# A mixture-of-experts layer and a state-space layer on one core: the 3x3 convolution on four 64x64 tiles of TensorE, one result row per token, part of softplus on TensorE, a Newton step on VectorE, and new slots for the side work

## The chip, the cores and the metric

The kernel runs on one NeuronCore of a Trainium2 chip. The core has engines that work at the same time, each through its own queue in order: TensorE (PE, matrix products into PSUM), VectorE (DVE), ScalarE (ACT), GpSimdE (POOL) and SyncE (SP, which only issues transfers here). They wait for one another by semaphores. The metric is device time in microseconds (us) of one execution; lower is better.

## The reference

The input is 32 images of 128 channels and 56x56 pixels, all in 32-bit floats. Two layers follow one another.

Layer 0 is a 7x7 depthwise convolution, a normalization over the channels, and a mixture of 8 experts of which each pixel ("token") uses its best two. Each expert is a two-layer network (128 to 512 to 128) with a capacity of 1.25 T/8 tokens. The result is input + normalized convolution + a small factor times the experts' weighted sum.

Layer 1 is what the change is mostly about. Cut to what matters (x is the result of layer 0, per image):

```python
xh = cv1_w @ x + cv1_b                                   # 1x1 convolution
l  = silu(batchnorm(depthwise_3x3(xh)))                  # the branch called lt in the kernel
t  = layernorm(xh over channels)                         # one token per pixel, in row order
xm, z = split(t @ in_proj_w.T)                           # 256 channels each
xm = silu(causal_conv4(xm))
dt, Bm, Cm = split(xm @ x_proj_w.T, [8, 24])             # 8, 16 and 16 columns
dt = softplus(dt @ dt_proj_w.T + dt_proj_b)              # 256 channels
for each token, each of 256 channels, each of 16 states:
    h = exp(dt * A) * h + dt * Bm * xm ;  y += h * Cm
g  = ((y + xm * D) * silu(z)) @ out_proj_w.T
out = x + cv2_w @ concat(l, g) + cv2_b
```

## The kernel before

**Layer 0.** The convolution runs on TensorE with banded weight matrices, and its normalized rows go to a table in memory, `res_d`. A routing stage on VectorE finds each token's two experts and its places. A dispatch stage copies token rows into `buf_d`, sorted by expert, with GpSimdE's indirect transfers (line 415). An expert stage (lines 434 to 496) reads `buf_d` in groups of four blocks of 112 tokens, multiplies, and adds each result row back into `res_d` with an indirect transfer that accumulates (line 464), four a group, 1,120 in all. `res_d` has 2T rows: the first T hold the normalized convolution, to which the result of a token's first choice is added; the other T rows are zeroed by 14 transfers (line 247) and take the second choice. All 1,120 transfers are declared independent of one another, as one group named "back".

**Layer 1** (function `layer1`) is software-pipelined by hand. Its order is kept as written. The work is cut into 224 groups `g` (32 images x 7 strips of 8 rows, 448 tokens) and each group into 16 units, one per state. Unit `u` needs, in this order:

- `db_pool` (line 948, POOL): db = du * Bm for both halves of the channels, 128x896;
- `exp_act` (line 954, ACT): da = exp(dt * A) in two instructions, into one of two PSUM buffers `da`;
- `scan_dve` (line 963, DVE): the recurrence over the 448 tokens of both halves, in place in `da`, or into an SBUF tile `hs` if the unit's number is in `POOL_C`;
- `cmul` (line 969): the product with Cm, on DVE, or for the five units of `POOL_C` on POOL;
- `carry_act` (line 975, ACT): the state at the strip's end is copied into db of the next strip (zeros at an image's last strip);
- `sum_pe` (line 911, PE): the product is added up over the 16 states, on four 64x64 tiles of TensorE at once.

The loop runs over `t`, one unit a step, and each step writes into the queues: POOL `cmul(t-1)` if it is POOL's; ACT `carry(t-1)`; POOL `db(t+4)`; ACT `exp(t+1)`; DVE `scan(t)` and its `cmul(t)`; PE, in odd steps, the sums of units t-3 and t-2; then the step's side work. So ACT is one unit ahead of DVE: `exp(t+1)` has to be done while DVE works on unit t. The number of a step within its group is i = t mod 16.

Side work is everything else of a group. Each piece is put at a fixed offset by `at(offset, function)`: with offset -15, `silus` of group g+1 stands in step i = 1 of group g, and so on. The pieces in their order: `moe_pe` (x + res_d, turned by a permutation), `cv1_pe`/`cv1_act` (the 1x1 convolution into `xh`, and squares for the variance), `var_pe`, `rstd_act` and `rstd_pool` (the inverse deviation, with a Newton step on POOL, lines 752 to 755), `bc_pe`, `te_dve` (normalized tokens, with the last three of the strip before copied on POOL, line 777), `xm_pe` (four products for each half, line 785), `silus` (lines 801 to 818: switch ACT's table, silu of xm, silu of the lt branch, silu of z, switch back), `px_pe`, `dt_pe`, the steps of softplus (`sp_abs`, `sp_exp`, `sp_r` on DVE, `sp_ln`, `sp_sub` on POOL at line 873, `sp_add` on DVE at line 877), `du_pool`, `lt_pe` (the 3x3 convolution as nine products with diagonal 128x128 matrices, line 890) and `lt_act` (line 898). When the 16 sums are done, `yz_dve` (line 903, i = 2, ahead of the step's scan) and `out_pe`, `out_act` finish the group.

PSUM is fully used: two `da` buffers of two banks, one accumulator `py` of two banks, and two banks that all other products take in turn (`mm_tile`); a product waits until the reader of the product two before it is done.

## Time and profile before

| what | value |
|---|---|
| time, median of 3 runs | 17951.65 us (17951.25 to 17956.85) |
| profiled execution | 17990.1 us, its span 17988.1 us, mean granted TensorE clock 0.872 |
| convolution, routing, dispatch (to the first expert group at 4552 us) | about 4550 us |
| experts (first to last line-464 transfer, 4572 to 6570 us) | about 2000 us |
| layer 1, first scan (6643 us) to the end | 11345 us, 50.6 us for each of 224 groups |
| DVE, ACT, POOL, PE busy between 12000 and 15000 us | 2774, 2159, 2883, 2679 of 3000 us |

A profile line of a group of instructions names line, engine, operation, output and inputs, number, busy time, mean duration in ns, and the idle time ahead of it with what ended that. A line of the timeline has start, duration, engine, line, operation, and in brackets the idle time before it and what ended it. Durations of one engine overlap a little, so the pace of an engine is read from start to start.

### The profile page before, as it was taken

How to read it: one execution, taken by the hardware profiler on the slowest of the kernel's cores; microseconds unless marked ns; L12 is line 12 of the kernel's file. 1: busy time of each engine (PE TensorE's matmuls, PEld its weight loads, DVE VectorE, ACT ScalarE, POOL GpSimd, SP SyncE). 2: the span in 40 equal slices, each digit the busy share in tenths (PEclk: the TensorE clock that was granted, in tenths of full speed). 3: DMA queues.
4: the chain of work that ended last, by engine and by line, in shares of the span. 5: the costliest groups of instructions: out<-in, count | busy, mean ns of one | idle time of the engine just before them, and what ended most of it. 6: DMA issues, size and time to landing. Idle time of an engine off the chain costs nothing. (4 is left out here: it accounts for less than half of the span.)

```text
span 17988.1 us, 212727 instructions
## 1 busy us (share of the span) xinstructions
PE 13659.5 (76%) x75556; PEld 7243.9 (40%) x75556; DVE 12454.2 (69%) x9483; ACT 9672.7 (54%) x18570; POOL 14710.8 (82%) x9375
## 2 busy tenths in 40 slices
PE   4887120000899988888888888888888888888888
PEld 3887100000677753333333333333333333333333
DVE  1766750000111139999999999999999999999999
ACT  2333000000344447777777777777777777777776
POOL 1333127777788879999999999999999999999999
PEclk8898555555999999999999999999999999999999
DMA  9778712222455545555555555555555555555554
GB/s 224 206 206 207 170 53 82 86 82 69 68 68 68 67 85 165 166 166 164 165 165 165 165 166 165 166 166 164 164 165 165 165 165 165 166 164 164 165 165 155
DMA packets 1567881, 2633.82 MB, mean 146 GB/s; under 512 B 145935, under 2 KB 1012603, under 8 KB 1562720
## 3 DMA queue, kind: packets, MB, share of 16 engines
q1 hardware_dynamic: 1368160, 2464.60, 46.8%
q0 software_dynamic: 198656, 155.62, 5.9%
q8 instruction: 595, 9.75, 0.2%
q14 instruction: 470, 3.85, 0.1%
HBM read 2231.69 MB, written 426.81 MB: 148 GB/s over the span
## 5 line engine op out<-in xcount | busy, mean ns | idle before, releaser
L948 POOL TENSOR_TENSOR db<-du,bb 128x896 f32<-128x896 f32 x3584 | 7416.5, 2092 | 0.1
L963 DVE TENSOR_TENSOR_SCAN da<-da,db 128x898 f32<-128x898 f32 x2464 | 4978.1, 2020 | 86.9 <-ACT da L954 86.8
L954 ACT ACTIVATE da<-dt,aneg 128x449 f32<-128x449 f32 x7168 | 4578.4, 639 | 584.0 <-DVE hs L963 244.6
L911 PE MATMUL py<-prod,ident 64*64 64x448 f32 x28672 | 3472.0, 599 | 116.3 <-POOL prod L969 104.4
L969 DVE TENSOR_TENSOR prod<-da,cb 128x896 f32<-128x896 f32 x2464 | 2689.7, 1092 | 196.7 <-issue 3.6
L969 POOL TENSOR_TENSOR prod<-hs,cb 128x896 f32<-128x896 f32 x1120 | 2321.2, 2073 | 389.2 <-issue 333.2
L963 DVE TENSOR_TENSOR_SCAN hs<-da,db 128x898 f32<-128x898 f32 x1120 | 2262.0, 2020 | 247.9 <-ACT db L975 210.6
L464 POOL DMA_INDIRECT res_d<-ys,xb x1120 | 1650.4, 1474 | 371.8 <-issue 304.6
L415 POOL DMA_INDIRECT buf_d<-xg,slot x1568 | 1535.9, 980 | 486.0 <-issue 476.7
L492 ACT COPY xc<-ept 128x448 f32<-128x448 f32 x280 | 149.0, 532 | 3010.7 <-DMA xb<-buf_d 2033.2
L911 PEld LDWEIGHTS py<-prod,ident 64*64 64x64 f32 x28672 | 981.7, 141 | 1941.7 <-issue 1118.7
L890 PE MATMUL p_l<-xh,dwd 128*128 128x448 f32 x4032 | 1748.1, 580 | 0.0
L490 PE MATMUL ept<-ident,xb 112*128 112x112 f32 x1120 | 200.0, 260 | 2032.7 <-DMA xb<-buf_d 2032.7
L785 PE MATMUL p_xm<-te,wk 128*128 128x448 f32 x3584 | 1415.8, 546 | 0.0
L412 DVE COPY xg<-gate 128x28 f32<-128x28 f32 x56 | 11.5, 232 | 1792.4 <-DMA buf_d<-xg,slot 1792.4
L456 DVE TENSOR_TENSOR ys<-py,b2t 112x512 f32<-112x512 f32 x280 | 193.6, 691 | 1521.6 <-PE py L451 1477.8
L890 PEld LDWEIGHTS p_l<-xh,dwd 128*128 128x128 f32 x4032 | 794.8, 208 | 958.5 <-issue 957.1
L451 PEld LDWEIGHTS py<-w2t,hh 128*112 128x112 f32 x8960 | 1031.1, 177 | 163.2 <-issue 114.8
L451 PE MATMUL py<-w2t,hh 128*112 128x128 f32 x8960 | 1094.9, 275 | 0.0
L175 PE MATMUL pc<-xc,toep 112*112 112x112 f32 (+1 forms) x8192 | 986.6, 280 | 108.0 <-ACT toep L164 66.1
L204 POOL TENSOR_TENSOR xa<-xa,lng 112x896 f32<-112x896 f32 x128 | 278.5, 2175 | 951.0 <-DVE xa L201 584.4
L735 PE MATMUL p_var<-mean_w,sq 128*112 128x1 f32 x1792 | 318.3, 299 | 906.5 <-ACT sq L720 906.5
(227 smaller groups left out, 19612.3 us busy)
## 6 DMA issues: line engine op xcount, KB each, us to landing
bb<-bc_d SPq DMA_DIRECT2D x1792, 448.0 KB
cb<-bc_d SPq DMA_DIRECT2D x1792, 448.0 KB
toep<-toep_d SPq DMA_DIRECT2D x448, 392.0 KB
xg<-res_d SPq DMA_DIRECT2D x56, 1792.0 KB
yg<-res_d SPq DMA_DIRECT2D x448, 224.0 KB
buf_d<-zero SPq DMA_DIRECT2D x14, 4550.0 KB
xb<-buf_d SPq DMA_DIRECT2D x280, 227.5 KB
xt<-in_x SPq DMA_DIRECT2D x32, 1568.0 KB
```

The source lines that it names most:

```text
L175: nc.tensor.matmul(pc[:, c, :, lo:hi], lhsT=tp[c // 2][:, c % 2, 6 - 2 * o : 8 - 2 * o, :], rhs=s4[:, c, :, lo + o - 1 : hi + o - 1], star ...
L415: apart(nc.gpsimd.indirect_dma_start(out=buf_d[:, :], out_offset=bass.IndirectOffsetOnAxis(ap=slots[k][:, q, p0 + j : p0 + j + 1], axis=0) ...
L451: nc.tensor.matmul(py[:, j, :], lhsT=hh[:, k, j * TT : (j + 1) * TT], rhs=w2t[:, k, :], start=k == 0, stop=k == KF - 1,)
L464: apart(nc.gpsimd.indirect_dma_start(out=res_d[:, :], out_offset=bass.IndirectOffsetOnAxis(ap=xb[:, j, C + 1 : C + 2].bitcast(I32), axis=0 ...
L735: nc.tensor.matmul(p[:TT, j : j + 1], lhsT=sq[:, j * TT : (j + 1) * TT], rhs=mean_w[:, 0:1], start=True, stop=True)
L785: nc.tensor.matmul(p[:, :CH1], lhsT=s["wk"][:, k, hs], rhs=d["te"][:, k : k + CH1], start=k == 0, stop=k == DC - 1 and not first,)
L890: nc.tensor.matmul(d["p_l"][:, :CH1], lhsT=s["dwd"][:, t, :], rhs=d["xh"][:, dy : dy + ROWS1, dx : dx + HW], start=t == 0, stop=t == 8,)
L911: nc.tensor.matmul(st[g]["py"][h * HD : (h + 1) * HD, r, :CH1], lhsT=lhsT(rs, h), rhs=rhs[rs, h, :], start=start, stop=stop,)
L948: nc.gpsimd.tensor_tensor(dbv[i][:, :, 1:], st[g]["du"], units[u].pop("bb"), ALU.mult)
L954: nc.scalar.activation(da[:, h * W1 : (h + 1) * W1], st[g]["dt"][:, h, :], AF.Exp, scale=s["aneg"][:, h, i : i + 1])
L963: nc.vector.tensor_tensor_scan(hs, da, dbs[i], 0.0, ALU.mult, ALU.add)
L969: eng.tensor_tensor(w["prod"], w["hs"][:, :, 1:], w.pop("cb"), ALU.mult)
```

## The change

1. `res_d` has T rows. Both choices of a token are added into the same row. The 14 zeroing transfers are gone, and the accumulating transfers are independent only within one expert (`back{e}`): those of expert e follow those of expert e-1. `fetch` reads one row per token, and `moe_pe` has 4 products instead of 8 besides the one for x.
2. `lt_pe` works on four 64x64 tiles: each tap has four products of a 64x64 diagonal block with 4 of the 8 image rows (224 columns), into two PSUM buffers; `lt_act` reads them with four instructions of 64x224, with the scale and bias turned to match (`bnt`).
3. Softplus: relu + ln are added on TensorE (`sp_pe`, two products with the identity for each half, four in all), and DVE subtracts the rounding rest from PSUM, one half at a time (`sp_sub`). POOL's subtraction and DVE's addition are gone.
4. The Newton step and the copy of three columns of `te` go from POOL to DVE.
5. `POOL_C` is now 2, 5, 8, 12, 14, `prod` has six buffers instead of five, and most of the side work has another slot: the silu phase moves from i = 1 to i = 0, `xm_pe` to 14 and 15, `sp_ln` to 7, `lt_pe` to 12 and 13, `lt_act` to 14, ahead of `xm_pe`.

```diff
-POOL_C = (0, 3, 7, 11, 14)
+POOL_C = (2, 5, 8, 12, 14)
...
-        res_d = dram.tile([2 * T, C], F32, name="res_d")
+        res_d = dram.tile([T, C], F32, name="res_d")
...
-        res_t = res_d.rearrange("(k p) c -> p k c", p=TT)
-        for k in range(COLS, 2 * COLS, 64):
-            nc.sync.dma_start(out=res_t[:, k : k + 64, :], in_=zero[:, :, :C].to_broadcast([TT, 64, C]))
...
-                nc.gpsimd.iota(bi, pattern=[[128 * TT, QB], [1, TT]], base=k * T, channel_multiplier=TT)
+                nc.gpsimd.iota(bi, pattern=[[128 * TT, QB], [1, TT]], base=0, channel_multiplier=TT)
...
-                        in_=ys[:, j, :], in_offset=None, bounds_check=2 * T - 1, oob_is_err=False, compute_op=ALU.add,
-                    ), "back")
+                        in_=ys[:, j, :], in_offset=None, bounds_check=T - 1, oob_is_err=False, compute_op=ALU.add,
+                    ), f"back{e}")
...
+            bnt = wp.tile([128, 2, 2], F32, name="bnt")
+            for k in range(2):
+                for r in range(2):
+                    for j, v in enumerate((bbi, bsc)):
+                        nc.scalar.copy(bnt[k * HD : (k + 1) * HD, r, j : j + 1], v[r * HD : (r + 1) * HD, :])
...
-            d["yg"] = two.tile([TT, TPC1, 2, C], F32, name="yg")
-            for k in range(2):
-                r = k * T + t0
-                nc.sync.dma_start(
-                    out=d["yg"][:, :, k, :], in_=res_d[r : r + CH1, :].rearrange("(j p) c -> p j c", p=TT)
-                )
+            d["yg"] = two.tile([TT, TPC1, C], F32, name="yg")
+            nc.sync.dma_start(
+                out=d["yg"], in_=res_d[t0 : t0 + CH1, :].rearrange("(j p) c -> p j c", p=TT)
+            )
...
-                for k in range(2):
-                    nc.tensor.matmul(
-                        p[:, j * TT : (j + 1) * TT], lhsT=yg[:, j, k, :], rhs=perm,
-                        start=False, stop=k == 1 and j == TPC1 - 1,
-                    )
+                nc.tensor.matmul(
+                    p[:, j * TT : (j + 1) * TT], lhsT=yg[:, j, :], rhs=perm, start=False, stop=j == TPC1 - 1
+                )
...
-        def rstd_pool(g):
+        def rstd_dve(g):
...
-            nc.gpsimd.tensor_tensor(w, r, r, ALU.mult)
-            nc.gpsimd.tensor_tensor(w, w, v, ALU.mult)
-            nc.gpsimd.tensor_scalar(w, w, -0.5, 1.5, ALU.mult, ALU.add)
-            nc.gpsimd.tensor_tensor(r, r, w, ALU.mult)
+            nc.vector.tensor_tensor(w, r, r, ALU.mult)
+            nc.vector.tensor_tensor(w, w, v, ALU.mult)
+            nc.vector.tensor_scalar(w, w, -0.5, 1.5, ALU.mult, ALU.add)
+            nc.vector.tensor_tensor(r, r, w, ALU.mult)
...
-                nc.gpsimd.tensor_copy(te[:, : DC - 1], st[g - 1]["te"][:, CH1:])
+                nc.vector.tensor_copy(te[:, : DC - 1], st[g - 1]["te"][:, CH1:])
...
-        def sp_sub(g):
-            d = st[g]
-            nc.gpsimd.tensor_tensor(d["u"], d["u"], d.pop("e"), ALU.subtract)
-
-        def sp_add(g):
-            d = st[g]
-            nc.vector.tensor_tensor(d["dt"][:, :, 1:], d["dt"][:, :, 1:], d.pop("u"), ALU.add)
+        def sp_pe(g, h):
+            d = st[g]
+            d[f"p_sp{h}"] = p = mm_tile("p_sp")
+            for k, v in enumerate((d["dt"][:, :, 1:], d["u"])):
+                nc.tensor.matmul(p[:, :CH1], lhsT=ident, rhs=v[:, h, :], start=k == 0, stop=k == 1)
+
+        def sp_sub(g, h):
+            d = st[g]
+            nc.vector.tensor_tensor(
+                d["dt"][:, h, 1:], d.pop(f"p_sp{h}")[:, :CH1], d["e"][:, h, :], ALU.subtract
+            )
...
-                d["p_l"] = mm_tile("p_l")
+                d["p_l"] = [mm_tile("p_l") for r in range(2)]
+            R = ROWS1 // 2
             for t in ts:
                 dy, dx = divmod(t, 3)
-                nc.tensor.matmul(
-                    d["p_l"][:, :CH1], lhsT=s["dwd"][:, t, :], rhs=d["xh"][:, dy : dy + ROWS1, dx : dx + HW],
-                    start=t == 0, stop=t == 8,
-                )
+                for r in range(2):
+                    rs = slice(r * HD, (r + 1) * HD)
+                    for k in range(2):
+                        nc.tensor.matmul(
+                            d["p_l"][r][k * HD : (k + 1) * HD, : CH1 // 2], lhsT=s["dwd"][rs, t, rs],
+                            rhs=d["xh"][rs, dy + k * R : dy + (k + 1) * R, dx : dx + HW], start=t == 0, stop=t == 8,
+                        )
...
-            d["lt"] = two.tile([C, CH1], F32, name="lt")
-            nc.scalar.activation(d["lt"], d.pop("p_l")[:, :CH1], AF.Identity, bias=s["bbi"], scale=s["bsc"])
+            lt = d["lt"] = two.tile([C, CH1], F32, name="lt")
+            ps = d.pop("p_l")
+            for r in range(2):
+                rs = slice(r * HD, (r + 1) * HD)
+                for k in range(2):
+                    ks = slice(k * HD, (k + 1) * HD)
+                    nc.scalar.activation(
+                        lt[rs, k * CH1 // 2 : (k + 1) * CH1 // 2], ps[r][ks, : CH1 // 2], AF.Identity,
+                        bias=s["bnt"][ks, r, 0:1], scale=s["bnt"][ks, r, 1:2],
+                    )
...
-            w["prod"] = three.tile([128, 2, CH1], F32, name="prod", bufs=5)
+            w["prod"] = three.tile([128, 2, CH1], F32, name="prod", bufs=6)
...
-        at(-35, moe_pe)
-        at(-34, moe_act)
+        at(-30, moe_pe)
+        at(-29, moe_act)
...
-        at(-22, rstd_pool)
-        at(-21, bc_pe)
-        at(-20, te_dve)
-        at(-17, xm_pe, 0)
-        at(-16, xm_pe, 1)
-        at(-15, silus)
-        at(-14, px_pe)
-        at(-13, px_act)
+        at(-23, rstd_dve)
+        at(-22, bc_pe)
+        at(-21, te_dve)
+        at(-2, lt_act)
+        at(-18, xm_pe, 0)
+        at(-17, xm_pe, 1)
+        at(-16, silus)
+        at(-15, px_pe)
+        at(-14, px_act)
         at(-12, dt_pe)
         at(-11, sp_abs)
         at(-10, sp_exp)
         at(-9, sp_r)
-        at(-8, sp_ln)
-        at(-7, sp_sub)
-        at(-6, sp_add)
+        at(-9, sp_ln)
+        at(-7, sp_pe, 0)
+        at(-6, sp_sub, 0)
+        at(-6, sp_pe, 1)
+        at(-5, sp_sub, 1)
         at(-5, du_pool)
-        at(-6, lt_pe, range(0, 5))
-        at(-5, lt_pe, range(5, 9))
-        at(-4, lt_act)
-        work.setdefault(DS * G - 15, []).append((silus, G))
+        at(-4, lt_pe, range(0, 5))
+        at(-3, lt_pe, range(5, 9))
+        work.setdefault(DS * G - 16, []).append((silus, G))
```

More of the change, by code (lines that the diff above doesn't have):

```diff
@@ L62, in tile_kernel @@
         buf_d = dram.tile([E * CAP, RW], F32, name="buf_d")
-        res_d = dram.tile([2 * T, C], F32, name="res_d")
+        res_d = dram.tile([T, C], F32, name="res_d")
         zero = const.tile([TT, 1, RW], F32, name="zero")
         nc.gpsimd.memset(zero, 0.0)
-        nc.gpsimd.memset(zero[:, :, C + 1].bitcast(I32), 2 * T)
+        nc.gpsimd.memset(zero[:, :, C + 1].bitcast(I32), T)
         ident = const.tile([128, 128], F32, name="ident")
@@ L436, in tile_kernel, with products @@
             todo = []
-            def products(g, xb, xc, w1t, w2t, b1t, b2t):
+            def products(e, g, xb, xc, w1t, w2t, b1t, b2t):
                 hh = eb.tile([128, KF, GT * TT], F32, name="hh")
@@ L494, in tile_kernel @@
                         products(*todo.pop())
-                    todo.append((g, xb, xc, w1t, w2t, b1t, b2t))
+                    todo.append((e, g, xb, xc, w1t, w2t, b1t, b2t))
             products(*todo.pop())
@@ L645, in layer1 @@
     mm_tile, res_d, x_d, out_d = s["mm_tile"], s["res_d"], s["x_d"], s["out_d"]
-    perm, T = s["perm"], s["T"]
+    perm = s["perm"]
     G = N * NQ1
```

## The prediction

> **What bounds the kernel now.** I began with the busy time of the engines in a stretch of layer 1 (core total; the columns are stretch, length, then PE, weight loads, DVE, ACT, POOL, TensorE clock, DMA share, GB/s):
>
> ```profile
> 12000.00:15000.00 3000.00, 2679.03 (x13541) 1145.26 (x13542) 2774.47 (x1836) 2158.96 (x4307) 2883.30 (x1676) 0.94 0.54 165
> ```
>
> POOL is busiest (96%), DVE next (92%). Which of them sets the pace is told by the waits between 8000 and 17000 us, some 178 groups (microseconds in total, times, longest):
>
> ```profile
> DVE yz L903 <- PE py L911: 262.1, 178, 2.2
> POOL prod L969 <- issue: 260.5, 319, 1.5
> ...
> ACT da L954 <- DVE hs L963: 193.6, 152, 1.6
> ...
> DVE hs L963 <- ACT db L975: 164.8, 157, 1.4
> ...
> DVE da L963 <- ACT da L954: 68.9, 152, 0.8
> ...
> DVE hs L963 <- POOL te L777: 2.6, 8, 0.3
> ```
>
> DVE waits for PE and ACT, some 2.95 us a group, and for POOL practically never. POOL in turn waits before its products; the timeline of POOL shows them starting just as DVE's scan ends. So the pace is DVE's own work plus its waits for PE and ACT, and POOL, full as it is, follows. The DVE timeline of one group shows the work and the waits:
>
> ```profile
> 12002.23 2.02 DVE L963 TENSOR_TENSOR_SCAN hs<-da,db 128x898 f32<-128x898 f32 x1
> ...
> 12011.31 1.09 DVE L969 TENSOR_TENSOR prod<-da,cb 128x896 f32<-128x896 f32 x1
> 12013.74 1.09 DVE L903 TENSOR_TENSOR yz<-py,zs 128x896 f32<-128x896 f32 x1 [1.34 <-PE py L911]
> ...
> 12018.97 2.03 DVE L963 TENSOR_TENSOR_SCAN hs<-da,db 128x898 f32<-128x898 f32 x1 [1.07 <-ACT db L975]
> ...
> 12030.22 2.02 DVE L963 TENSOR_TENSOR_SCAN hs<-da,db 128x898 f32<-128x898 f32 x1
> 12032.16 1.07 DVE L865 SCALAR_TENSOR_TENSOR sp_e<-sp_u,sp_e 128x896 f32<-128x896 f32 x1
> 12033.67 2.04 DVE L963 TENSOR_TENSOR_SCAN da<-da,db 128x898 f32<-128x898 f32 x1 [0.45 <-ACT da L954]
> ...
> 12052.71 2.02 DVE L963 TENSOR_TENSOR_SCAN hs<-da,db 128x898 f32<-128x898 f32 x1
> ```
>
> First and last row are unit 14 of two groups: 50.48 us. From start to start a unit with its product takes 3.11 us, a unit whose product is POOL's 1.94, sp_r, sp_add and yz 1.0 each, te 0.53. Work: 11 x 3.11 + 5 x 1.94 + 3 x 1.0 + 0.53 = 47.4. The rest, 3.0, is three stalls: 2.4 around ACT's silu phase (1.34 + 1.07), 0.45 before unit 8, and small gaps. The second shows a mechanism that matters below; the ACT timeline:
>
> ```profile
> 12030.86 0.14 ACT L975 COPY db<-da 128x2 f32<-128x2 f32 x1
> 12032.27 1.31 ACT L954 ACTIVATE da<-dt,aneg 128x449 f32<-128x449 f32 x2 [1.27 <-DVE hs L963]
> ```
>
> exp(8) was put into the buffer that scan(7) reads, not the one unit 6 had left, so it starts only as scan(7) ends, and scan(8) starts 3.45 us after scan(7) did (30.22 to 33.67) instead of 1.94. sp_r fills 1.0 of the 1.5.
>
> **The change part by part** (per group; there are 224).
>
> *DVE's work.* sp_add goes (-1.0). Two halves of sp_sub come, each like te (448 columns from PSUM): 2 x 0.55. The four Newton instructions depend on one another; such small ones in the preparation of layer 1 follow at 0.19 if dependent (lines 558 to 560) and at 0.07 if not: 0.75, bounds 0.3 and 1.1. The copy of `te` 0.1. Sum +0.95, bounds +0.5 and +1.4.
>
> *POOL's work.* Gone: 2.04 (line 873), about 1.85 from the first Newton instruction to the next db, 0.15 (line 777). Worth nothing by itself: DVE lost 2.6 us in 9000 to POOL.
>
> *The buffers of exp.* In the built order of the changed program exp(6) waits for scan(5) and exp(9) for scan(8), in 191 of 224 groups (those of an image's last strip, whose carry is zeros, wait for the products of units 4 and 7 instead). No DVE work stands between the scans now, since sp_r follows unit 7. Each place takes 3.45 instead of 1.94: +1.5 twice. ACT then lags: from scan(5) as zero, exp(6) 2.05, sp_abs 3.3 to 5.4 (four at 0.515), exp(7) 5.5, sp_exp and its sum to 8.55; scan(6) 3.45, scan(7) 6.88 (0.3 late), sp_r to 11.0; exp(8) 8.75, cv1_act to 11.3, sp_ln (moved here) 12.1; scan(8) 11.0, exp(9) 13.05, scan(9) 14.45. DVE's work in that is 11.1: stalls 3.3 against 0.45, +2.9. In the 32 last strips only ACT's lateness is left, about 1.25: +0.8. Behind the waiting exps stand sp_abs and carry(7), and cv1_pe and var_pe wait for them; both have over 2 us to spare.
>
> *lt on tiles.* The rows have no tile product of 224 columns. Four of 448 at once (line 911) take 0.83 a set; half the columns take between 0.42 and 0.83. My estimate is 0.46, as stream time halves and 0.08 of overhead stays (the value nearest to the row that is of the same form): nine taps 4.1 instead of 7.1 (12039.49 and 12046.15, 10 and 8 instructions). moe_pe saves 0.9, sp_pe adds four products at 0.78, 3.1. PE's total stays at about 43 of 50 us; it matters only through xm_pe.
>
> *The silu phase.* Now at step 0. lt starts after te and sp_sub's second half on DVE (both PSUM buffers are theirs), at the start of scan(12); with 4.1 for lt and 1.7 for sums it ends 5.8 later, ahead of lt_act, which ACT reaches 6.6 after scan(12). xm_pe now needs the PSUM buffers that lt_act reads: its first half starts 7.3 after scan(12), 3.1; sums 1.7; second half 3.1, ending 15.1 after scan(12), which is 5.0 after unit 15 (1.94 + 3.11 + 1.94 + 3.11 = 10.1). ACT: exp(1) 0.3 after unit 15, table 1.55 to 2.85, silu xm to 3.4, waits for xm's second half to 5.1, silus and z to 7.5, table 8.8, exp(2) 9.0, scan(2) 10.4. DVE's work in between is two units and yz, 7.2: stall 3.1 to 3.2 against 2.4, +0.7. The sums before yz now follow z on PE, but end 8.5 after unit 15, inside this stall. If xm were in time, ACT alone would set 8.7: stall 1.5, -0.9. If lt gains nothing from tiles, all this is 2.5 later.
>
> *lt_act.* Row: one instruction of 448 columns has a pace of 0.62; copies of 56 columns have 0.13 and others of 448 0.515, so by estimate 224 cost 0.295 and four 1.18. It stands after exp(15) and ends before exp(0) is due: hidden by unit 14, and if late it adds to the line above. "TensorEngine Tiling (Array Packing)" of the Trainium skill, PSUM Bottleneck, says that tiling speeds up TensorE but not the emptying of PSUM. By that alone the reading would stay at 0.62 and release xm 0.28 earlier; the rows say that it nearly doubles.
>
> *The other moves.* moe_pe, now 1.8 us, stands at step 2 behind px_pe and ahead of dd and the sums of units 0 and 1; out_pe then ends 5.3 us after scan(3) starts, dt_pe 1.8 later, and sp_abs needs it 2.4 later still, after the late exp(6). bc_pe waits for DVE's Newton step after unit 9, the second sp_pe for the first sp_sub after unit 10; behind them are sums and lt, which start no later than te and the second sp_sub allow. While xm_pe waits for lt_act, sums of units 12 and 13 stand behind it, needed only by yz. SP issues one `yg` transfer less a group; SP held up nothing. A sixth `prod` buffer: DVE waited once, 0.5 us, for one. All nothing; their cover is DVE's own work of 3.1 us a step, and with it gone each would cost what it is late.
>
> *Outside layer 1.* The zeroing ran at 1912 to 2103 us beside the routing on DVE, and SP then waited 404 us for routing: worth 0 to 30 us (DVE waited 30.7 for row stores at the end of the convolution), I take 10. The first add of an expert now waits for the last of the one before: the last of all landed about 1.8 us after POOL had issued it (6570.95 to 6572.75), so about 1.5 seven times, with the expert's other adds behind it on POOL; six `ys` buffers keep DVE and PE going. POOL's adds take 7.03 of each 7.13 us of the PE-bound stage, so little of it is made up: +10. Preparation, first and last group: as before.
>
> Sum: 192 groups x (0.95 + 2.9 + 0.7) + 32 x (0.95 + 0.8 + 0.7) = 874 + 78 = 952 us, less 10, plus 10: 950. The profiled execution (17990, span 17988) would go to 18940; it was 38 above the median of the runs, so the time is 17952 + 950 = 18900.
>
> **Rivals.** *A, PE becomes late* (15%): tile products of 224 columns are bound by weight loads and issue, or run at a lower clock. For it: in the trace, after PE idled 4.27 us, 16 tile products took 3.26 us instead of 1.73, and I expect several gaps of 2 to 3 us in steps 7 to 12. Against: each gap is shorter than that. With +2.5: 18900 + 560 = 19460. *B, the silu stall shrinks* (23%): xm is ready when ACT wants it, as in the profile, where ACT waits 5.2 us for it in 178 groups together. Against: lt_act now stands before xm. -0.9 for +0.7: 18900 - 360 = 18540. *C, faster, by POOL* (4%): if the full POOL queue is the true limit and the DVE waits only mirror it, a group falls to DVE's work of 48.35, -2.1 x 224: 17480. It decides if all stalls left are under 2.1 us a group; the two exp waits alone are 3.0, so the program's waits would have to be met in time, and the same one now is not (152 times 1.27). *D, parts cancel* (2%): 17950.
>
> **How the numbers follow.** The forecast itself has 56%: 18900, its own range 18700 to 19150. The lowest bound of the slower cases is 0.5 + 2.6 - 0.9 = 2.2 in 192 groups, 18360; the highest 1.4 + 3.1 + 0.7 + 2.5 = 7.7, about 19600. I give 18440 to 19460. A measurement tells 0.2% (36 us) from no change: faster 0.045, same 0.015, slower 0.94.
>
> **What would show it.** In the profile after: scan(5) to scan(6) and scan(8) to scan(9) 3.45 apart, with exp waiting for the scan; ACT waiting over 1 us for xm; line-900 products near 4 us a group; POOL with 6 us or more idle in each group; a group of 55 us. I am wrong if DVE's stalls stay near 3 us, or if lt takes 7 us.

## The result, and the profile after

The changed kernel takes 19794.04 us (median of 3 runs, 19790.33 to 19802.44), 1.1026 times the kernel before (95% interval 1.1004 to 1.1047). The forecast was 18900 in a range of 18440 to 19460: slower was right, but the loss is 1842 us and not 950. Its profiled execution has a span of 19800.5 us.

The same stretch of layer 1 as shown of before (length; then PE, weight loads, DVE, ACT, POOL, clock, DMA share, GB/s):

```profile
12000.00:15000.00 3000.00, 2410.88 (x14409) 1044.61 (x14408) 2620.28 (x1880) 1935.40 (x3859) 2256.69 (x1143) 0.87 0.43 138
```

POOL went from 2883 to 2257 us busy, 48.5 to 44.1 us a group (the forecast took 4.0 off), and the kernel gains nothing by it. DVE looks less busy than before (2774), but a part of its 2620 us is no work, as will be seen. TensorE's granted clock is lower, 0.87 against 0.94, and it was busy for 80% of the time instead of 89%. A group took 50.5 us; from unit 8 of one group to unit 8 of the next it is now 58.67.

Where DVE and POOL wait, between 8000 and 17000 us (153 groups; total, times, longest):

```profile
DVE yz L921 <- PE py L929: 430.5, 153, 5.1
DVE da L981 <- ACT da L972: 430.4, 427, 1.8
DVE hs L981 <- ACT db L993: 102.8, 134, 1.1
...
POOL du L887 <- DVE dt L880: 1273.8, 152, 8.8
```

The second line is the stall by exp's buffers (before: 68.9 in 178 groups), the first and third are the silu phase. ACT's timeline has both causes: exp waits for the scan, and in the silu phase ACT waits for the second half of xm, which TensorE starts late because its first half waits for `lt_act` (line 913) to read the buffers (the last fence is TensorE's):

```profile
12054.47 1.31 ACT L972 ACTIVATE da<-dt,aneg 128x449 f32<-128x449 f32 x2 [1.77 <-DVE hs L981]
...
12088.43 2.17 ACT L913 ACTIVATE lt<-p_l,bnt 64x224 f32<-64x224 f32 x4
...
12097.73 0.63 ACT L802 ACTIVATE xm<-p_xm,c1b 128x448 f32<-128x448 f32 x1 [2.22 <-PE p_xm L786]
```

```profile
12089.55 3.27 PE L786 MATMUL p_xm<-te,wk 128*128 128x448 f32 x8 [1.92 <-ACT lt L913]
```

POOL now stands idle 8.4 us a group for DVE. The timeline of DVE shows both stalls as forecast, 3.45 us from the scan of unit 8 to that of unit 9 and 2.68 + 0.77 around yz, and behind the product of unit 9 something that was not:

```profile
12063.52 2.02 DVE L981 TENSOR_TENSOR_SCAN hs<-da,db 128x898 f32<-128x898 f32 x1
12066.97 2.04 DVE L981 TENSOR_TENSOR_SCAN da<-da,db 128x898 f32<-128x898 f32 x1 [1.43 <-ACT da L972]
12069.09 1.09 DVE L987 TENSOR_TENSOR prod<-da,cb 128x896 f32<-128x896 f32 x1
12070.10 1.59 DVE L753 TENSOR_TENSOR rw<-r 112x4 f32<-112x4 f32 x1
12071.72 1.99 DVE L754 TENSOR_TENSOR rw<-rw,v 112x4 f32<-112x4 f32 x1
12073.75 0.17 DVE L755 TENSOR_SCALAR rw<-rw 112x4 f32<-112x4 f32 x1
12073.95 0.16 DVE L756 TENSOR_TENSOR r<-r,rw 112x4 f32<-112x4 f32 x1
...
12101.17 1.09 DVE L921 TENSOR_TENSOR yz<-py,zs 128x896 f32<-128x896 f32 x1 [2.68 <-PE py L929]
12103.03 2.03 DVE L981 TENSOR_TENSOR_SCAN hs<-da,db 128x898 f32<-128x898 f32 x1 [0.77 <-ACT db L993]
```

Lines 753, 754 and 756 are the same operation on 4 columns, yet take 1.59, 1.99 and 0.16 us. No idle time is shown before them: the wait is inside the instruction. POOL's timeline over the same stretch:

```profile
12067.55 6.14 POOL L966 TENSOR_TENSOR db<-du,bb 128x896 f32<-128x896 f32 x3
```

Three products db, 2.05 us each, end at about 12069.6, 12071.7 and 12073.7. Line 753 ends with the second, line 754 with the third, and then POOL has nothing to do and line 756 is quick. The means over all groups say the same, and in some groups line 755 waits too (number, busy time, mean ns):

```profile
L754 DVE TENSOR_TENSOR rw<-rw,v 112x4 f32<-112x4 f32 x153 | 305.0, 1993 | 5.3
L753 DVE TENSOR_TENSOR rw<-r 112x4 f32<-112x4 f32 x153 | 218.3, 1427 | 0.0
L866 DVE SCALAR_TENSOR_TENSOR sp_e<-sp_u,sp_e 128x896 f32<-128x896 f32 x152 | 216.8, 1426 | 0.0
...
L755 DVE TENSOR_SCALAR rw<-rw 112x4 f32<-112x4 f32 x153 | 66.2, 433 | 5.2
L756 DVE TENSOR_TENSOR r<-r,rw 112x4 f32<-112x4 f32 x153 | 24.9, 163 | 5.2
```

DVE's time per group, from the totals of its instructions and waits, divided by 178 groups before and 153 after:

| us a group | before | after | difference | forecast |
|---|---|---|---|---|
| Newton step on DVE | 0 | 4.02 | +4.02 | +0.75 |
| sp_add, or the halves of sp_sub and te's copy | 1.15 | 1.37 | +0.2 | +0.2 |
| sp_r | 1.07 | 1.43 | +0.36 | 0 |
| wait for exp (units 6, 7, 9; before: 8) | 0.39 | 2.81 | +2.4 | +2.6 |
| silu phase: waits before yz and the next scans | 2.53 | 3.57 | +1.0 | +0.7 |
| sum | | | +8.0 | +4.25 |

The measured difference is 1842/224 = 8.2 us a group. (The forecast of 2.6 is 2.9 in 192 groups and 0.8 in 32.)

### The profile page after: what moved, and what is told of

Same layout as the page of the kernel before. It is cut to its first block, busy times and chain, and to the rows that moved or that the text cites. A ratio compares the mean times of both kernels' runs of the same rounds, so it can differ in the third digit from the quotient of the medians.

```text
span 19800.5 us, 237405 instructions
## 1 busy us (share of the span) xinstructions
PE 14124.6 (71%) x87652; PEld 7511.8 (38%) x87652; DVE 13481.3 (68%) x10795; ACT 10009.0 (51%) x19249; POOL 13723.4 (69%) x8063
## 5 line engine op out<-in xcount | busy, mean ns | idle before, releaser
L929 PE MATMUL py<-prod,ident 64*64 64x448 f32 x28672 | 3540.4, 614 | 18.6 <-POOL prod L987 11.5
L987 POOL TENSOR_TENSOR prod<-hs,cb 128x896 f32<-128x896 f32 x1120 | 2163.5, 1932 | 1386.0 <-PE p_moe L698 701.1
L929 PEld LDWEIGHTS py<-prod,ident 64*64 64x64 f32 x28672 | 1051.0, 148 | 2068.9 <-issue 1567.4
L887 POOL TENSOR_TENSOR du<-dt,xm 128x896 f32<-128x896 f32 x224 | 432.2, 1930 | 1908.4 <-DVE dt L880 1882.5
L786 PE MATMUL p_xm<-te,wk 128*128 128x448 f32 x3584 | 1477.0, 555 | 325.4 <-ACT lt L913 323.3
L993 ACT COPY db<-da 128x2 f32<-128x2 f32 x2112 | 335.4, 159 | 2349.7 <-DVE prod L987 2342.8
L763 PE MATMUL p_bc<-ident,r 112*128 112x112 f32 x1792 | 430.5, 418 | 1073.7 <-DVE r L756 1073.7
L786 PEld LDWEIGHTS p_xm<-te,wk 128*128 128x128 f32 x3584 | 645.9, 190 | 1076.6 <-issue 712.9
```

The source lines that it names most:

```text
L763: nc.tensor.matmul(p[:, j * TT : (j + 1) * TT], lhsT=r[:, j : j + 1].to_broadcast([TT, 128]), rhs=ident[:TT, :TT], start=True, stop=True,)
L786: nc.tensor.matmul(p[:, :CH1], lhsT=s["wk"][:, k, hs], rhs=d["te"][:, k : k + CH1], start=k == 0, stop=k == DC - 1 and not first,)
L887: nc.gpsimd.tensor_tensor(d["du"], d["dt"][:, :, 1:], d["xm"], ALU.mult)
L929: nc.tensor.matmul(st[g]["py"][h * HD : (h + 1) * HD, r, :CH1], lhsT=lhsT(rs, h), rhs=rhs[rs, h, :], start=start, stop=stop,)
L987: eng.tensor_tensor(w["prod"], w["hs"][:, :, 1:], w.pop("cb"), ALU.mult)
```

## The experiments

Ratios are to the kernel before, run beside each kernel on the same chip; 0.01 of ratio is 180 us, or 0.80 us for each of the 224 groups. Where a kernel is an edit of the changed one, it is compared with that one's ratio of 1.1026. Two theories stand against each other at first: P, that the Newton step's instructions on DVE wait for POOL's instruction under way, and D, that they cost what was forecast and the loss lies elsewhere.

### The Newton step

**e1: back on POOL**, all four instructions, at the same place of the changed kernel.

```diff
-            nc.vector.tensor_tensor(w, r, r, ALU.mult)
+            nc.gpsimd.tensor_tensor(w, r, r, ALU.mult)
...
```

> The changed kernel, with the four Newton instructions back on POOL, in the same place of the order. Theory P (on VectorE the two tensor_tensor whose inputs all lie in SBUF wait for the POOL instruction that is under way): all of the 3.7 us that VectorE spends on them leaves each group, 224 x 3.7 = 830 us, so 18960 us; and POOL, which now idles 8.4 us a group, has room for its 1.85. Rival D (four small dependent instructions cost 0.75 as forecast, the rest of the loss is TensorE and its lower clock): 19794 - 170 = 19620. Rival S (POOL's Newton step stands behind long products and makes bc and te late): no gain, 19800 or more.

Measured: 18917.08 us, ratio 1.0514 (1.0497 to 1.0532). That is 4.1 us a group less than the changed kernel, all that lines 753 to 756 took. Theories D and S fall. On POOL each of the four took 0.20 us.

**e2: the same step on DVE, one input in PSUM.** This keeps engine, place and count, and changes only where r lies.

```diff
-            nc.scalar.activation(d["r"], d["r"], AF.Exp, scale=-0.5)
+            nc.scalar.activation(p[:TT, 64 : 64 + TPC1], d["r"], AF.Exp, scale=-0.5)
...
-            nc.vector.tensor_tensor(w, r, r, ALU.mult)
-            nc.vector.tensor_tensor(w, w, v, ALU.mult)
+            nc.vector.tensor_tensor(w, rp, v, ALU.mult)
+            nc.vector.tensor_tensor(w, rp, w, ALU.mult)
             nc.vector.tensor_scalar(w, w, -0.5, 1.5, ALU.mult, ALU.add)
-            nc.vector.tensor_tensor(r, r, w, ALU.mult)
+            nc.vector.tensor_tensor(r, rp, w, ALU.mult)
```

> The changed kernel, with the Newton step still on VectorE and in its place, but the first estimate r is written to PSUM, so that each of the three tensor_tensor has one input in PSUM and one in SBUF (w = r*v, w = r*w, r*w; as many instructions as before). Theory P: nothing waits for POOL any more, the step falls from some 3.7 us to 0.75 at most, 224 x 2.9 = 650 us less: 19140 us. Rival D (the time is the instructions' own, or their dependence): unchanged, 19794 within 100. Rival S (the slot of PSUM that r now holds longer makes bc late): slower than 19794.

Measured: 19341.89 us, ratio 1.0750 (1.0732 to 1.0768), 2.2 us a group less, where P had said 2.9. The groups of DVE in this kernel tell why:

```profile
L756 DVE TENSOR_SCALAR rw<-rw 112x4 f32<-112x4 f32 x159 | 169.5, 1066 | 5.5
L757 DVE TENSOR_TENSOR r<-p_var,rw 112x4 f32<-112x4 f32 x159 | 25.7, 162 | 5.5
L755 DVE TENSOR_TENSOR rw<-p_var,rw 112x4 f32<-112x4 f32 x159 | 25.7, 162 | 5.5
L754 DVE TENSOR_TENSOR rw<-p_var,v 112x4 f32<-112x4 f32 x159 | 24.1, 152 | 0.0
```

The three with an input in PSUM never wait: 152 to 162 ns in all 159 groups. The one with a single input, input and output both in SBUF, takes over: 1066 ns in the mean, 174 at the least. So one input and one output in SBUF can be enough to wait; two inputs there are not needed.

**e6: no instruction left that has only SBUF operands.**

```diff
             nc.vector.tensor_tensor(w, rp, v, ALU.mult)
-            nc.vector.tensor_tensor(w, rp, w, ALU.mult)
-            nc.vector.tensor_scalar(w, w, -0.5, 1.5, ALU.mult, ALU.add)
-            nc.vector.tensor_tensor(r, rp, w, ALU.mult)
+            nc.vector.scalar_tensor_tensor(w, w, -0.5, rp, ALU.mult, ALU.mult)
+            nc.vector.scalar_tensor_tensor(r, w, 1.5, rp, ALU.add, ALU.mult)
```

> The changed kernel with the Newton step on VectorE in three instructions, each with one input in PSUM (w = r*v, w = -0.5*w*r, r = (w + 1.5)*r with r in PSUM): the instruction with one input and a constant, which still waited (median 1.2 us) when the other three no longer did, is gone. Theory P: it was waiting for POOL too; three instructions of 0.16 without a wait, 1.2 us a group less than 19342: 19070 us. Rival D (it costs that by itself, or a wait goes to the next one): 19342, or 0.17 a group less, 19300.

Measured: 19244.09 us (19083.76 to 19255.9), ratio 1.0656 (1.0580 to 1.0732). The three took 152, 158 and 157 ns in the mean; none waits, and the whole step takes 0.47 us instead of 4.02. The time is another 0.8 us a group lower than in e2 (the interval is wide); the wait before yz is 0.1 us a group larger.

The page "SBUF — State Buffer" of the Trainium skill, section "Who interferes with whom", says that VectorE and GpSimd share one pair of SBUF ports under an exclusive lock, held for a whole instruction: a VectorE instruction with two SBUF inputs contends with a GpSimd instruction that reads SBUF, and so can `tensor_scalar` and copies, in a mode that uses both ports. These three runs agree with it, in both kinds (1.99 against 0.16 us; 1.07 against 0.17 us).

**e4: the step on DVE alone, in the kernel before** (lines 752 to 755 from `nc.gpsimd` to `nc.vector`, nothing else).

> The kernel before, with nothing changed but the engine of the Newton step: VectorE instead of POOL. Theory P: two of its instructions wait for the POOL instruction under way, 1 to 2 us each, and VectorE sets the pace, so 3 to 3.8 us a group: 17952 + 670 to 850, 18620 to 18800 us. Rival D: 0.75 a group, 18120 us. Rival G (POOL set the pace, and gains 1.85 a group): 17550 to 17950.

Measured: 18323.64 us, ratio 1.0183 (1.0166 to 1.0200): +1.5 us a group, between D and P. The mechanism is P's, the amount is not:

```profile
L753 DVE TENSOR_TENSOR rw<-rw,v 112x4 f32<-112x4 f32 x172 | 323.8, 1882 | 5.9
L752 DVE TENSOR_TENSOR rw<-r 112x4 f32<-112x4 f32 x172 | 55.9, 325 | 0.0
```

With the other two (0.17 and 0.16) this makes 2.5 us a group. The first instruction mostly finds POOL between two products (its median is 152 ns). And 1.4 us come back: the wait before yz, 262.1 us in 178 groups before, is 4.2 here, as DVE reaches yz later, while that before the following scans rises from 1.06 to 1.56 a group. The same step thus costs 1.5 us in the one kernel and 4.1 in the other.

### The two buffers of exp

**e3: POOL's products in the old units.**

```diff
-POOL_C = (2, 5, 8, 12, 14)
+POOL_C = (0, 3, 7, 11, 14)
```

> The changed kernel with the products on POOL in units 0, 3, 7, 11, 14 again instead of 2, 5, 8, 12, 14. In the built order exp(8) then waits for scan(7), and neither exp(6) for scan(5) nor exp(9) for scan(8): one such place instead of two. Theory B (each place costs 1.5 us, and sp_r stands in the one that is left): 1.5 for the place that goes and 1.0 for sp_r in the other, 2.5 us a group, 19794 - 560 = 19230 us. Rival O (ACT's lateness and the silu phase take it back): 19600 to 19800.

Measured: 19636.18 us, ratio 1.0914 (1.0896 to 1.0932), 0.9 us a group less, where B had said 2.5. The wait for exp did go, from 430.4 to 72.4 us. But 2.6 us of waits for TensorE came in its place:

```profile
DVE yz L921 <- PE py L929: 697.5, 155, 6.2
DVE dt L880 <- PE p_sp L876: 142.1, 155, 1.0
```

4.5 us a group before yz against 2.8, and 0.9 before the second half of sp_sub: TensorE isn't early enough for a DVE that comes earlier, as rival O had it. These waits are more than the 2.3 us of stalls that went. What made the kernel faster all the same is that DVE's instructions meet POOL's less: sp_r is back at 1.07 us (from 1.43), and the Newton step takes 3.3 us instead of 4.0.

**e5: the buffers in turn.** Units stay where they are; only the choice of buffer changes.

```diff
-            da = units[u]["da"] = pda.tile([128, 1024], F32, name="da")
+            da = units[u]["da"] = pda.tile([128, 1024], F32, name="da", tag=f"da{u % 2}", bufs=1)
```

> The changed kernel, with one difference: the two PSUM buffers of exp are given to even and odd units in turn, so that in the built order no exp waits for the scan of the unit just before it. Theory B: both stalls of 1.43 us on VectorE go, 2.9 us a group, 19794 - 640 = 19150 us. Rival O (units 6 to 9 come earlier, but the silu phase, which waits for TensorE, does not, and takes it back as it did with the products of POOL moved): 19550 to 19750 us, with VectorE's wait before yz 1.5 us a group or more above the 2.8 of the changed kernel.

Measured: 19970.48 us (19823.97 to 19974.78), ratio 1.1060 (1.0985 to 1.1134): nothing is gained, and neither theory had that. The stall is gone (22.7 us left of 430.4, and 78.3 of other waits in its place), and the silu phase is as it was (2.9 a group before yz). What grew are DVE's instructions in SBUF:

```profile
L866 DVE SCALAR_TENSOR_TENSOR sp_e<-sp_u,sp_e 128x896 f32<-128x896 f32 x153 | 443.5, 2899 | 0.0
L755 DVE TENSOR_SCALAR rw<-rw 112x4 f32<-112x4 f32 x153 | 306.9, 2006 | 5.2
L754 DVE TENSOR_TENSOR rw<-rw,v 112x4 f32<-112x4 f32 x153 | 305.2, 1995 | 5.3
```

sp_r from 1.43 to 2.90, line 755 from 0.43 to 2.01, line 753 down to 0.46: 2.1 us of 2.2 gained are waited again, now behind POOL. Starting earlier, DVE meets more of POOL's products.

**e10: both**, e5's buffers and e6's Newton step.

> The changed kernel with two things: the three-instruction Newton step on VectorE that never waits, and the two buffers of exp in turn. Theory B2 (the buffers' stalls are 2.8 us a group; alone, their end only brought sp_r and the Newton step under POOL's instructions): with the Newton step out of that, 2.8 go and sp_r gives 1.9 back, 0.9 a group, 19240 - 200 = 19040 us, sp_r at a mean of 2.5 to 3 us. Rival O (the silu phase takes what is left too): 19200 to 19300, sp_r at a mean near 1.1.

Measured: 18872.04 us, ratio 1.0489 (1.0471 to 1.0506), 1.3 us a group below e6 (0.7 to 2.0 by e6's interval), a little more than the 0.9 of theory B2. sp_r takes 2.89 us in the mean, as B2 said. So of the 2.8 us a group that the stalls had, a part can be had, once the Newton step is out of POOL's way.

**e11: the same in the kernel before**, where one stall of 0.45 us is left.

> The kernel before with the two buffers of exp in turn, nothing else. Theory B: the stall of 0.45 us before unit 8 goes, 154 + 27 of 224 groups, 17990 - 85 = 17905 us. Rival K (sp_r, which now starts earlier against POOL's long instructions, waits for one of them, 0.5 to 1.9 us, as it did in the changed kernel): 18050 to 18300 us, with sp_r at a mean above 1.5 us.

Measured: 18098.37 us, ratio 1.0059 (1.0042 to 1.0075), slower. K holds, with another instruction than the one it named: sp_r stays at 1067 ns; sp_add, which also has both inputs in SBUF, rises from 1159 to 1603, and the waits around the silu phase by 0.4 us together.

### What the parts on TensorE are worth

**e7: lt not on tiles**, in the changed kernel (functions `lt_pe` and `lt_act` as before, slots as changed).

```diff
-                        nc.tensor.matmul(
-                            d["p_l"][r][k * HD : (k + 1) * HD, : CH1 // 2], lhsT=s["dwd"][rs, t, rs],
-                            rhs=d["xh"][rs, dy + k * R : dy + (k + 1) * R, dx : dx + HW], start=t == 0, stop=t == 8,
-                        )
+                nc.tensor.matmul(
+                    d["p_l"][:, :CH1], lhsT=s["dwd"][:, t, :], rhs=d["xh"][:, dy : dy + ROWS1, dx : dx + HW],
+                    start=t == 0, stop=t == 8,
+                )
```

> The changed kernel with lt not on tiles but as before (nine products of 448 columns into one bank, one instruction for lt_act), in its new place of the order. Theory L (lt on tiles is what keeps the silu phase short): lt takes 7.1 us instead of 3.7 and xm ends 2 to 3 us later, 19794 + 450 to 670 = 20240 to 20460 us. Rival T (the wait is for the buffer that lt_act reads, and one short lt_act gives it back sooner; or lt lies in other stalls): 19600 to 19900 us.

Measured: 20481.21 us, ratio 1.1354 (1.1275 to 1.1434): 2.6 us a group slower, as L said and as the forecast had it for this case (2.5). The timeline of TensorE in this kernel, then in the changed one:

```profile
12030.08 4.03 PE L895 MATMUL p_l<-xh,dwd 128*128 128x448 f32 x10
12035.70 3.27 PE L895 MATMUL p_l<-xh,dwd 128*128 128x448 f32 x8
```

```profile
12082.54 2.07 PE L900 MATMUL p_l<-xh,dwd 64*64 64x224 f32 x40
12085.94 1.69 PE L900 MATMUL p_l<-xh,dwd 64*64 64x224 f32 x32
```

7.3 us against 3.8 for the nine taps. The Newton step and sp_r are as in the changed kernel (4.0 and 1.42 us), so the loss is not theirs. It is in the waits: ACT now waits for lt itself, 4.1 us a group (595.4 us in 146 groups; 0.1 a group in the changed kernel), and DVE for what ACT then does late, 2.4 us a group:

```profile
DVE da L968 <- ACT db L980: 350.5, 131, 3.0
```

**e13: softplus' sum on TensorE alone**, in the kernel before.

```diff
-        at(-7, sp_sub)
-        at(-6, sp_add)
+        at(-8, sp_pe, 0)
+        at(-7, sp_sub, 0)
+        at(-7, sp_pe, 1)
+        at(-6, sp_sub, 1)
```

> The kernel before with one part of the change alone: sp_pe and sp_sub in halves (sp_pe at steps 8 and 9, sp_sub at 9 and 10) in place of sp_sub on POOL and sp_add on VectorE. As forecast (VectorE's work +0.1 us a group, POOL's 2 us worth nothing): 17990 + 0 to 40. Rival C (POOL's load sets the pace): 1 us a group less, 17770. Rival T (3 us more of TensorE at steps 8 and 9 make bc and lt late, as te's wait for bc in the mix showed): 18100 to 18400.

Measured: 18553.82 us, ratio 1.0307 (1.0290 to 1.0324): +2.5 us a group for a DVE that has no more to do and a POOL that has 2 us less. Rival C is out; T is right in kind, and larger than it said. ACT's wait for lt, between 8000 and 17000 us, in the kernel before and in this one (178 and 169 groups):

```profile
ACT lt L898 <- PE p_l L890: 396.5, 178, 3.5
```

```profile
ACT lt L902 <- PE p_l L894: 876.7, 169, 5.5
```

2.2 us a group become 5.2. TensorE gets some 3 us more to do ahead of lt, ACT waits for lt at step 12, its exps for units 14 and 15 stand behind, and DVE waits for those (2.6 us a group against 1.06). `te` waits 0.6 us a group for bc besides (100.4 us in 169 groups), which it did not before.

**e18: softplus' sum back on POOL and DVE**, within the changed kernel with e1's Newton step.

```diff
-        at(-7, sp_pe, 0)
-        at(-6, sp_sub, 0)
-        at(-6, sp_pe, 1)
-        at(-5, sp_sub, 1)
+        at(-7, sp_sub)
+        at(-6, sp_add)
```

> The changed kernel with the Newton step on POOL (as e1, 1.051 of the kernel before), and with sp_sub on POOL and sp_add on VectorE again in place of the halves on TensorE; lt on tiles, moe, POOL's units and all other slots stay. Theory T (the sums on TensorE cost 2.5 us a group there too): 18917 - 560 = 18360 us. Theory L (the shorter lt has paid for them: TensorE waits for lt_act in the silu phase anyway): 18917 within 60. Rival K (sp_add, with both inputs in SBUF, waits for POOL): 19100 or more.

Measured: 19822.56 us, ratio 1.1017 (1.0999 to 1.1036): 4.0 us a group slower than e1, where T had expected 2.5 less. K, in its plainest form; DVE and POOL in one group:

```profile
12041.97 4.46 DVE L878 TENSOR_TENSOR dt<-dt,sp_u 128x896 f32<-128x896 f32 x1
...
12050.01 0.60 DVE L778 COPY te<-te 128x3 f32<-128x3 f32 x1
```

```profile
12041.36 4.11 POOL L962 TENSOR_TENSOR db<-du,bb 128x896 f32<-128x896 f32 x2
...
12048.51 2.08 POOL L962 TENSOR_TENSOR db<-du,bb 128x896 f32<-128x896 f32 x1
```

sp_add, 1.1 us of work, takes 4.46 (mean 4.52 in 153 groups) and ends 0.96 after POOL's second product. The same section of the page "SBUF — State Buffer" of the Trainium skill says that whoever issues first gets the ports; here DVE, waiting since 12041.97, was passed by a product that started at about 12043.4. The measurement decides: a wait can outlast the product under way. (Line 753 above did get in between two products; why `sp_add` did not is not shown.) A copy of three columns takes 0.60 instead of 0.16, with its end at the end of a db. So the same edit that costs 2.5 us in the kernel before saves 4.0 in this order of the changed one (without its Newton step), where sp_add would stand beside POOL's products, while the halves read PSUM and wait for nobody.

**e9 and e17: one row per token alone**, in the kernel before, with moe in its new slot (e9) and in its old one (e17).

```diff
-        at(-35, moe_pe)
-        at(-34, moe_act)
+        at(-30, moe_pe)
+        at(-29, moe_act)
```

and, in both, part 1 of the change.

> The kernel before with one part of the change alone: one row per token for both experts, and moe_pe and moe_act at steps 2 and 3 instead of 13 and 14. Theory M (in the kernel before, moe's 2.9 us of TensorE at step 13 stand ahead of xm_pe and make xm, z and the sums late in the silu phase; VectorE waits 1.3 us there for the sums): xm_pe starts 1.7 us earlier, the wait before yz goes and the wait for the next exp grows by at most 0.3: 1.1 us a group, 17990 - 250 = 17740 us. Rival F (as I forecast: moe's place and size are worth nothing): 17990 within 40. Rival P (POOL, at 96 %, becomes the bound): 17900 or more with POOL's idle time below 0.3 us a group.

> The kernel before with one row per token for both experts, moe_pe and moe_act left at steps 13 and 14. Theory M, size: moe_pe is 0.9 us shorter and xm_pe, right behind it on a TensorE that does not idle there, starts 0.9 earlier: about half of e9's gain or a little more, 17995 - 110 to 200 = 17800 to 17885 us. Theory M, place alone: unchanged, 17995.

Measured: 17771.95 us, ratio 0.9875 (0.9859 to 0.9892), and 17785.44 us, ratio 0.9888 (0.9871 to 0.9904). Both beat both kernels; against the kernel before they gain 1.0 and 0.9 us a group, and their intervals overlap. The first scan came at 6656 and 6627 us, against 6643 before, so nearly all of the gain is layer 1's. The waits of DVE in e9 and e17 (182 and 181 groups):

```profile
DVE hs L954 <- ACT db L966: 255.8, 157, 2.0
...
DVE hs L954 <- ACT da L945: 38.1, 25, 1.5
```

```profile
DVE hs L954 <- ACT db L966: 179.9, 164, 1.5
DVE yz L894 <- PE py L902: 99.7, 175, 1.3
```

The size does it: in e17 four products less, 0.9 us of TensorE ahead of xm_pe, and the wait before yz falls from 1.47 to 0.55 a group. The new place in e9 takes the rest of that wait too, but it comes back as a wait for ACT before the next scans (1.6 us against 1.1): in the silu phase TensorE and ACT are late by nearly the same.

### Versions meant to be faster

Five more kernels, on the theory that the kernel before is left with DVE's own work and DVE's few stalls.

**e12** is e9 with e5's buffers.

> The kernel before with both: one row per token with moe at steps 2 and 3, and the two buffers of exp in turn. Theories M and B together: 1.1 + 0.4 us a group, 17990 - 335 = 17655 us. If sp_r waits for POOL (rival K): 17800 to 18050 us.

Measured: 17765.76 us, ratio 0.9874 (0.9857 to 0.9890), as e9 within the intervals: the stall of 0.39 us is gone, but sp_add took half of it (1352 ns in the mean against 1146) and 0.16 us a group is left as other waits before the scans.

**e14** is e9 with other units on POOL:

```diff
-POOL_C = (0, 3, 7, 11, 14)
+POOL_C = (3, 7, 9, 12, 14)
```

> The kernel with moe's part alone (e9), and the five products of POOL in units 3, 7, 9, 12, 14 instead of 0, 3, 7, 11, 14. Theory Z (in the silu phase VectorE waits 1.6 us for ScalarE, so a product of unit 0 on VectorE costs nothing there, and one less elsewhere saves 1.1): 17772 - 240 = 17530 us, with the wait for exp in the silu phase near 0.5. Rival P (POOL has its products closer together, becomes late, and VectorE waits for db, or waits behind it in sp_add): 17800 to 18100.

Measured: 18543.02 us, ratio 1.0306 (1.0289 to 1.0323), 3.5 us a group slower than e9 with no work added anywhere. sp_add in DVE's groups, and POOL's product of unit 9 and the db behind it in its timeline (sp_add started at 12041.20 there and took 2.12):

```profile
L868 DVE TENSOR_TENSOR dt<-dt,sp_u 128x896 f32<-128x896 f32 x170 | 373.3, 2196 | 0.0
```

```profile
12040.44 1.94 POOL L960 TENSOR_TENSOR prod<-hs,cb 128x896 f32<-128x896 f32 x1
12042.33 2.94 POOL L939 TENSOR_TENSOR db<-du,bb 128x896 f32<-128x896 f32 x1
```

1.05 us is sp_add behind POOL's product of unit 9 (and POOL behind sp_add: a db of 2.94 instead of 2.09). The rest is in waits for ACT and before yz (3.7 us a group together against 1.6 in e9); what made those longer was not tried apart.

**e8, e15 and e16** put a sixth product on POOL in place of sp_sub, with the sum on TensorE as in e13 (e8: both halves of sp_pe at step 9, of sp_sub at 10). e8 has e5's buffers and units 0, 3, 5, 8, 12, 14; e15 has e9's moe and units 0, 3, 7, 9, 12, 14; e16 is as e15 with units 3, 7, 9, 11, 12, 14.

> The kernel before, with three things: half of softplus' sum on TensorE as in the change (both halves of sp_pe at step 9, of sp_sub at step 10), the 2 us that this frees on POOL used for a sixth product there (units 0, 3, 5, 8, 12, 14), and the two buffers of exp in turn. Theory V (VectorE's own work sets the pace, and POOL has room): 1.17 less for the product, 0.1 more for sp_sub, 0.45 less for the stall before unit 8, 1.5 us a group: 17990 - 340 = 17650 us. Rival O (POOL, still at about 48 of 49 us a group, or the silu phase takes it back): 17900 to 18100 us.

> The kernel with moe's part alone (e9), with softplus on TensorE in halves as in e13, and a sixth product on POOL (units 0, 3, 7, 9, 12, 14). Theory V (VectorE's work 1.0 less a group, POOL's load as before): 17772 - 220 = 17550 us. Rival T (bc, lt and xm late by the added 3 us of TensorE): 17800 to 18200.

> As e15, with the six products of POOL in units 3, 7, 9, 11, 12, 14, so that unit 0's is VectorE's. Theories V and Z together: 17772 - 220 - 240 = 17310 us. Rival P (POOL, with five products and du within eight steps, is late): 17700 or more, with VectorE waiting for db.

Measured: 18579.1 us, ratio 1.0311 (1.0254 to 1.0368); 18320.7 us, 1.0174 (1.0157 to 1.0191); 18883.87 us, 1.0489 (1.0472 to 1.0507). All are slower than the kernel before. DVE had 1 us less work a group in each. In e8 ACT waited 5.1 us a group for lt, as in e13; in e16 DVE waited 2.0 us for bc and 4.1 for ACT around the silu phase. No kernel is clearly better than e9; e12 and e17 lie beside it.

## Why the prediction was right or wrong

**Where it failed: the Newton step.** "The four Newton instructions depend on one another; such small ones in the preparation of layer 1 follow at 0.19 if dependent (lines 558 to 560) and at 0.07 if not: 0.75, bounds 0.3 and 1.1." They cost 4.0 us in the trace and 4.1 in e1, 3.3 more than taken, of the 3.75 by which the table's two sums differ. The term was a price for the instructions alone; what the runs showed in its place is that they wait for POOL's instructions. The price came from a place where POOL was idle (it had nothing to do from 6570.95 to 6592.11 us, and lines 558 to 560 ran at 6575). The row that would have told was in the profile of before: POOL's own four Newton instructions took 1041, 234, 193 and 199 ns in the mean for the same 4 columns, and the "1.85 from the first Newton instruction to the next db" was put down as POOL's work:

```profile
L752 POOL TENSOR_TENSOR rw<-r 112x4 f32<-112x4 f32 x177 | 184.2, 1041 | 0.0
```

In the timeline the first of them ends with DVE's sp_add (12044.21 and 12044.15 us). In e1, where no DVE instruction with all operands in SBUF runs beside them, they take 0.20 each. And "DVE waits for PE and ACT, some 2.95 us a group, and for POOL practically never" took the list of waits for complete. A wait of this kind is not in it; on DVE in the kernel before it shows only in sp_add, with a mean of 1.16 us, a median of 1.08 and a longest of 1.62. The upper bound should have been a whole POOL instruction, 2.05, for each of the four at the least (e18 shows that a wait can be longer).

**sp_r**, priced at nothing, is 0.36 longer for the same reason: its median is 1.16 us, but some take 3.0, as that at 12767.50 us, which ends 0.95 after POOL's third db in a row.

**The buffers of exp** were right: +2.9 in 192 groups and 0.8 in the others, 2.6 as a mean, against 2.4 measured, with 3.45 us from scan to scan and exp waiting for the scan, as it was described. That the price is there does not mean that removing the cause returns it (e3, e5).

**The silu phase** was right in its mechanism and a little small: ACT waits 2.2 us for the second half of xm, and xm waits for lt_act; the stall is 3.45 us (2.68 + 0.77) in the typical group against a forecast of 3.1 to 3.2. **lt on tiles**: 4.1 forecast, 3.8 measured, 0.42 us for a set of four. That is half of the 0.83 of a set of 448 columns; the 0.08 that the estimate let stay as overhead shows in no run. **lt_act**: four instructions at 0.295 were forecast as 1.18, they took 2.17 (0.53 each for 64x224, where one of 448 columns had a pace of 0.62), so halving the columns hardly shortened them. Before DVE's scans it stayed hidden; what it added to the wait for xm was not tried apart.

**"All nothing"** for moe and sp_pe held for the sum but not for its parts: "PE's total stays at about 43 of 50 us; it matters only through xm_pe". Moe's shorter product is worth 0.9 us a group in the kernel before (e17), the sum on TensorE costs 2.5 (e13). TensorE was idle for 5.4 us a group (2679 of 3000 us busy), but 4.0 of that stood ahead of var_pe at step 8 (718.7 us in 178 groups), and only little between there and the silu phase, where both parts lie.

**Outside layer 1**: the first scan came at 6613 us in the changed kernel, at 6646 in e1, which is the same program up to there, at 6643 before. The forecast of +10 - 10 lies within that spread of 33 us, so these two terms are neither confirmed nor refuted.

**Rivals.** A: no; the clock fell, but the tile products took 3.8 us, less than the estimate, and a half of xm only 0.13 us longer. B: no; the silu stall grew. C: POOL did get 8.4 us idle and it was worth nothing; e13 shows it once more. D: no. "A group of 55 us", the last sign named, fits e1, which has no Newton step on DVE: 54.55 (12001.94 to 12056.49, from unit 12 to unit 12). That e1's 18917 us lie so near to the forecast of 18900 is luck: without the 0.75 of the step the sum gives a group of 54.0, and sp_r and the silu phase are each some 0.4 us above it.

## What to carry to other kernels

When POOL and VectorE both work all the time, sort VectorE's instructions by where their operands lie: those with an input in PSUM ran at their own pace here, those with all operands in SBUF could wait for POOL, whatever their size. A small instruction moved onto VectorE must then be bounded by a whole instruction of POOL, and where POOL's instructions follow one another without a gap, by more than one (e18). The cheap remedy here was to let one of its inputs lie in PSUM (e6). And where three engines are late by nearly the same, a stall that is removed comes back elsewhere: of the kernels that took a visible stall or one of VectorE's products away (e3, e5, e8, e10, e11, e12, e14, e15, e16), none gained more than about half of it, and the one sure gain on the kernel before came from less work on the engine that the others waited for (e17; e9 and e12 contain it).

## What the runs showed of the hardware that was not expected

- VectorE's wait for POOL shows nowhere as idle time: VectorE counts as busy for all 4.0 us a group of the Newton step, though four instructions of 0.16 would be 0.6, and only the spread of equal instructions (0.16 to 1.99 us) tells.
- It is not one instruction long at most: 4.5 us for a 1.1 us addition behind two products of 2.05 (e18). An instruction with one input and a constant waits too (1.07 us against 0.17, e2), and a copy of three columns (0.60 against 0.16, e18).
- It works in both directions: POOL's db took 2.94 us instead of 2.09 behind VectorE's addition (e14).
- TensorE's granted clock between 12000 and 15000 us differed from kernel to kernel: 0.94 before and in e13, 0.87 in the changed kernel, 0.84 in e18, with TensorE busy for 89, 91, 80 and 77% of the time. The share alone does not tell the clock: e16 had 89% and 0.91, e7 81% and 0.90. In the changed kernel a half of xm took 3.27 us instead of 3.14.
